# An LSTM over 512 steps in three gate banks instead of two, paired statistics, norms on GpSimd, and a total spread by matmuls

## The chip, the cores and the metric

The kernel runs on one core of one Trainium2 chip. Its time is the device time in microseconds (us) of one execution; less is better. The core's engines are PE (TensorE: matmuls into PSUM, with PEld for loading weights), DVE (VectorE), ACT (ScalarE), POOL (GpSimd) and SP (SyncE, which here issues DMAs). Each engine works through its own queue in order; semaphores tie the queues together.

## The reference, cut to what matters

Two layers are computed on `x` of 32 batches x 512 nodes x 256 features. Everything but the last block (two graph attentions and a state space block) is left as it is by the change. The last block is an LSTM that runs over the 512 nodes, all 32 batches side by side, followed by gated running sums:

```python
def _L1_ffn_ref(x, W_ih, W_hh, b_ih, b_hh, W_lin, b_lin, fw_att, bw_att):   # x is layer-normed
    x_proj = einsum('btd,gd->btg', x, W_ih) + b_ih + b_hh
    def step(carry, xp):
        h, c = carry
        i, f, g, o = split(xp + h @ W_hh.T, 4, axis=-1)
        c = sigmoid(f) * c + sigmoid(i) * tanh(g)
        h = sigmoid(o) * tanh(c)
        return (h, c), h
    lstm_out = scan of step over t
    logits = einsum('bth,lh->btl', lstm_out, W_lin) + b_lin      # two logits
    g = argmax(logits, axis=-1)[..., None]                        # 0 or 1
    w = g * lstm_out
    inc = cumsum(w, axis=1)
    prefix, suffix = inc - w, inc[:, -1:, :] - inc
    return 2.0 * lstm_out + prefix * fw_att + suffix * bw_att
x = x + _L1_ffn_ref(_layernorm(x), ...)
```

`suffix` needs the total over all steps, so a term of every output row is known only when the last step is done.

## The kernel before, in words

Two passes over the batches compute all that comes before the LSTM and leave the result in device memory as `X3` (512 steps x 32 batches x 256). Then `recurrence` runs.

*Layout.* The 256 hidden units are cut into four quarters (`Q` = 4) of 64 (`J`), and a quarter into two halves of 32 (`H`). The 128 partitions hold quarter x batch (4 x 32), so that a gate of one half is 32 columns wide. A step's gates are a PSUM tile pair `pg`: `pg0` has g, f, i of the first half (96 columns), `pg1` has g, f, i of the second half, o of both, and two columns of which the first is the logits' difference (162 columns). `z` is a row of columns of 32: 0 is the state c of the first half, 1 to 3 its gates, 4 the state of the second half, 5 to 7 its gates, 8 and 9 o of both, 10 and 11 tanh(c).

*A step t*, in the order in which the queues of PE, DVE and ACT are written (this part of the kernel is scheduled by hand: program order is queue order on those three engines; SP's and POOL's order is the scheduler's):

- PE: `part(pg, whh, h, ...)` adds h @ W_hh to the gates, for each pair (k, n) of an order, k being the half of h that is the stationary operand and n the gate bank, with one matmul for each of the four quarters. Then `x_part(t + 1, ...)` starts the next step's gates from x. In steps 5, 6, 10 and 11 of a chunk PE also transposes one normed tile of x for the next chunk (`turn`).
- ACT: tanh of `pg0` (L1472), tanh of `pg1` without the logits (L1473), then two tanh(c), one for each half (L1483), a copy of one column (L1485), and, after a transposition, the copy of it out of PSUM (L1356). Sigmoids are made of tanh by scaling the weights by a half.
- DVE: for each half `ab` (L1478) and the new c in `z2` (L1481), then for each half `hh` (L1491) and its 32 x 32 block transposition `h` (L1495), which the next step's matmuls load as weights. Then `g` (L1502, the logit decides whether h counts), one *extra* piece of work, and `pp` (L1508), the running sum.

*Chunks and extras.* 16 steps (`CH`) are a chunk. At its first step the lists of extra work are made; each step takes one entry. Before the change there are 16: four `stats` of the next chunk's x (one tile of 128 rows each: BATCH_NORM_STATS2 and BATCH_NORM_AGGREGATE; the last also gives POOL `rstd_of`, that is `ve` and the power `rs`), two pairs of `norm` (TENSOR_SCALAR on DVE in place, and a POOL memset of the last column), and ten pieces of the former chunk's `results` (128 x 512 adds and products on DVE; the last issues four DMAs on SP that gather the piece into `R`). At a chunk's first step `pp` is also copied (L1510).

*Memory.* `R` (128 partitions x 128 steps x 256) stays in SBUF and collects everything but the total. Its partitions are quarter of the steps x batch.

*The tail.* After the last step `tot` = total x `bw` (128 x 64, quarter x batch on partitions). Sixteen DMAs on three queues lay it out as `tots` (128 x 256, the four quarters of the columns side by side, repeated for the four quarters of the steps). The last chunk's ten result pieces run on DVE, then 17 adds `R` + `tots` in blocks of 2, 6 and 8 steps, each followed by four output DMAs on SP and ACT.

Of the kernel before, what the change touches and what calls it, by code (L numbers as in the profile page):

```python
# [9 lines left out]
F32 = mybir.dt.float32  # L10
# [3 lines left out]
AF = mybir.ActivationFunctionType  # L14
# [5 lines left out]
P = 128  # L20
# [1269 lines left out]
def recurrence(ctx, tc, c, a, X3, wr, out):  # L1290
# [25 lines left out]

    TQ = T // 4
    R = wp.tile([P, TQ, D], F32, name="R")


    NX = CH // 4

    def normalised(t0, out_):


        mv = small.tile([P, NX, 2], F32, tag="mv", name=f"mv{t0}")
        rs = [None]
        xs = []
        for n in range(NX):
            xt = xp_.tile([P, D], F32, tag=f"xt{n}", bufs=1, name=f"xt{t0}_{n}")  # L1330
            nc.sync.dma_start(out=xt, in_=X3[t0 + 4 * n : t0 + 4 * n + 4].rearrange("t b d -> (t b) d"))
            xs.append(xt)

        def stats(n):
            bs = small.tile([P, 6], F32, tag="bs", name=f"bs{t0}_{n}")
            nc.vector.bn_stats(bs, xs[n])
            nc.vector.bn_aggr(mv[:, n, :], bs)  # L1337
            if n == NX - 1:
                rs[0] = rstd_of(nc, small, c, mv[:, :, 1], NX, LN_EPS)

        def norm(n):
            nc.vector.tensor_scalar(
                xs[n], xs[n], mv[:, n, 0:1], rs[0][:, n : n + 1], ALU.subtract, ALU.mult
            )
            nc.gpsimd.memset(xs[n][:, D - 1 :], 1.0)

        def turn(n):
# [10 lines left out]
        return tuple([lambda f=f, n=n: f(n) for n in range(NX)] for f in (stats, norm, turn))  # L1358

    def results(t0, hh, pp):  # L1360

# [56 lines left out]
    def x_part(t, xT):  # L1418

        pg = [psg.tile([P, e - s], F32, tag=f"pg{n}", name=f"pg{n}_{t}") for n, (s, e) in enumerate(PARTS)]  # L1420
        r = (t % G) * GB
        part(pg, wih, [xT[t % CH // G][:, k, r : r + GB] for k in range(DK)], ((0, 0), (1, 0), (0, 1), (1, 1)), True, t == 0)
        return pg

    with tc.manual_schedule(engines={mybir.EngineType.PE, mybir.EngineType.DVE, mybir.EngineType.Activation}):
        nxt = [None] * 2
        stats, norms, turns = normalised(0, nxt)
        for s, e in ((0, nw), (n0, n0 + 2 * J + 1), (nw, n0)):
            nc.sync.dma_start(out=wall[:, s:e], in_=wr[:, s:e])
        for f in stats + norms:  # L1430
            f()
        for f in turns:
            f()()
        extra, turning = [], {}
        pg = x_part(0, nxt)


        z = st.tile([P, 12 * H + 1], F32, tag="z", name="z0")
        for n in range(2):
            nc.vector.memset(z[:, 4 * n * H : (4 * n + 1) * H], 0.0)  # L1440
        pp = ch.tile([P, CH + 1, J], F32, tag="pp", name="pp0")
        nc.vector.memset(pp[:, 0, :], 0.0)
        h = hh = None
        for t in range(T + 1):
            s = t % CH
            last = t == T
            if s == 0 and not last:
                t0 = t
                hh_was, pp_was = hh, pp
                hh = ch.tile([P, CH, J], F32, tag="hh", name=f"hh{t0}")  # L1450
                if t:
                    pp = ch.tile([P, CH + 1, J], F32, tag="pp", name=f"pp{t0}")
                assert not extra and not turning
                xT, nxt = nxt, [None] * 2
                stats, norms, turns = normalised(t0 + CH, nxt) if t0 + CH < T else ([], [], [])
                more = results(t0 - CH, hh_was, pp_was) if t else []
                both = [lambda fs=norms[n : n + 2]: [f() for f in fs] for n in range(0, len(norms), 2)]
                extra = stats + both + more
                turning = {(5, 6, 10, 11)[n]: f for n, f in enumerate(turns)}
            if last:  # L1460

                pg = [None, psg.tile([P, W - 3 * H], F32, tag="pg1", name="pglast")]
                part(pg, whh, h, ((0, 1), (1, 1)), True, True)
            elif t:
                part(pg, whh, h, ((0, 0), (0, 1), (1, 0), (1, 1)), False, True)
            pgs = pg
            if not last:
                if t + 1 < T:
                    pg = x_part(t + 1, xT if t + 1 < t0 + CH else nxt)
                turned = [turning.pop(s)()] if s in turning else []  # L1470

                nc.scalar.activation(z[:, H : 4 * H], pgs[0], AF.Tanh)  # L1472
                nc.scalar.activation(z[:, 5 * H : 10 * H], pgs[1][:, : 5 * H], AF.Tanh)  # L1473
                z2 = st.tile([P, 12 * H + 1], F32, tag="z", name=f"z{t + 1}")
                for n in range(2):
                    c0 = 4 * n * H
                    ab = st.tile([P, 2 * H], F32, tag=f"ab{n}", name=f"ab{n}_{t}")
                    nc.vector.scalar_tensor_tensor(  # L1478
                        ab, z[:, c0 + 2 * H : c0 + 4 * H], 1.0, z[:, c0 : c0 + 2 * H], ALU.add, ALU.mult
                    )  # L1480
                    nc.vector.scalar_tensor_tensor(z2[:, c0 : c0 + H], ab[:, :H], 0.5, ab[:, H:], ALU.mult, ALU.add)  # L1481
                for n in range(2):
                    nc.scalar.activation(z[:, (10 + n) * H : (11 + n) * H], z2[:, 4 * n * H : (4 * n + 1) * H], AF.Tanh, scale=0.5)  # L1483

                nc.scalar.copy(z2[:, 12 * H :], level)  # L1485
                for f in turned:
                    f()
                h = []
                for n in range(2):
                    half = hh[:, s, n * H : (n + 1) * H]  # L1490
                    nc.vector.scalar_tensor_tensor(  # L1491
                        half, z[:, (8 + n) * H : (9 + n) * H], 1.0, z[:, (10 + n) * H : (11 + n) * H], ALU.add, ALU.mult
                    )
                    h.append(st.tile([P, GB], F32, tag=f"h{n}", name=f"h{n}_{t}"))
                    nc.vector.transpose(h[n], half)  # L1495
                z = z2
            if t:

                i = (t - 1) % CH
                p_, h_ = (pp_was, hh_was) if s == 0 and not last else (pp, hh)  # L1500
                g_ = st.tile([P, J], F32, tag="g", name=f"g{t}")
                nc.vector.scalar_tensor_tensor(  # L1502
                    g_, pgs[1][:, 5 * H : 5 * H + 1].to_broadcast([P, J]), level, h_[:, i, :], ALU.is_gt, ALU.mult,
                )
            if extra and not last:
                extra.pop(0)()
            if t:
                nc.vector.tensor_tensor(p_[:, i + 1, :], p_[:, i, :], g_, ALU.add)  # L1508
# [4 lines left out]
        nc.vector.tensor_tensor(tot, pp[:, CH, :], bw, ALU.mult)  # L1513

        tots = wp.tile([P, D], F32, name="tots")
        for n in range(4 * Q):
            tq, q = n // Q, n % Q
            (nc.sync, nc.scalar, nc.gpsimd)[n % 3].dma_start(
                out=tots[tq * GB : (tq + 1) * GB, q * J : (q + 1) * J], in_=tot[q * GB : (q + 1) * GB]
            )  # L1520
        for f in results(T - CH, hh, pp):
            f()
        t0 = 0
        for step in [2, 6] + [8] * (TQ // 8 - 1):
            r = R[:, t0 : t0 + step, :]
            nc.vector.tensor_tensor(r, r, tots.unsqueeze(1).to_broadcast([P, step, D]), ALU.add)  # L1526
            for tq in range(4):
                (nc.sync, nc.scalar)[tq % 2].dma_start(
                    out=out[:, tq * TQ + t0 : tq * TQ + t0 + step, :], in_=r[tq * GB : (tq + 1) * GB]
                )  # L1530
            t0 += step


PERIOD, PIECES = 100234, 49
# [121 lines left out]
```

## Time and profile before

| | |
|---|---|
| median of 3 runs (range) | 3854.9 us (3853.66 to 3856.93) |
| the profiled execution's own time | 3853.91 us |
| its span, first to last instruction | 3852.2 us |
| mean granted PE clock | 0.975 |
| busy in the span: PE, DVE, ACT, POOL | 3417.8, 3256.5, 2403.0, 1510.6 us |
| first activation of the first step (L1472) | 2550.76 us |
| `tot` (L1513), after the last step | 3786.76 us |
| first and last add to `R` (L1526) | 3793.84 to 3829.2 us |

The span is the stretch from the first to the last instruction; the 1.7 us by which the execution is longer lie around it. The recurrence with its tail takes the last third. In it, by windows of the trace (busy us of each engine in a stretch):

| stretch, us | PE | DVE | ACT | POOL | DMA share |
|---|---|---|---|---|---|
| 2900 to 3100 (steady steps) | 171.18 | 187.19 | 98.41 | 9.41 | 0.22 |
| 3787 to 3794 | 0.00 | 6.73 | 0.00 | 2.57 | 0.10 |
| 3794 to 3829 | 0.00 | 35.00 | 0.00 | 0.00 | 0.96 |
| 3829 to 3852.2 | 0.00 | 0.21 | 0.00 | 0.00 | 0.86 |

The groups of the recurrence that the change touches, from the table of costliest groups with shapes kept apart (count, mean of one):

| group | count | mean ns |
|---|---|---|
| L1413 PE matmul, 96 columns, with h | 8128 | 252 |
| L1413 PE matmul, 162 columns, with h | 8128 | 301 |
| L1472 ACT tanh, 128x96 | 508 | 251 |
| L1473 ACT tanh, 128x160 | 509 | 305 |
| L1336 DVE BATCH_NORM_STATS2, 128x256 | 121 | 418 |
| L1337 DVE BATCH_NORM_AGGREGATE | 121 | 182 |
| L1342 DVE TENSOR_SCALAR norm, 128x256 | 124 | 406 |
| L1378 to L1390 DVE result pieces, 128x512 | 320 | 681 |
| L1518 `tots` DMAs | 16 | - |

An fp32 matmul appears as two records in the trace, so a step has 32 matmul records with h and 32 with x. Matmuls that work on different quarters overlap; a "mean of one" is therefore no measure of how often they can follow each other. The timeline of single steps tells that: rows are in order of start, with the length, and in brackets the idle time of that engine before and what released it.

### The profile page before, as it was taken

What the parts mean: (1) busy time and instruction counts of PE and PEld (TensorE: products, weight loads), DVE (VectorE), ACT (ScalarE), POOL (GpSimd) and SP (SyncE); (2) the same over time, 40 slices, a digit from 0 to 9 for tenths busy, and PEclk for the clock granted to TensorE, in tenths of its full rate; (3) what the DMA queues carried; (4) which work ended last, traced back from release to release, by engine and by line L of the source; (5) the groups of instructions that cost most, each with busy time, mean ns of one, the idle gap of its engine ahead of it and who ended that gap; (6) DMA issues with size and microseconds to landing.
All of it is one profiled execution on the core that took longest, in us unless ns stands there. A gap on an engine that the chain in (4) does not pass through costs nothing. (4 is left out here: it accounts for less than half of the span.)

```text
span 3852.2 us, 117182 instructions
## 1 busy us (share of the span) xinstructions
PE 3417.8 (89%) x47370; PEld 2313.5 (60%) x47370; DVE 3256.5 (85%) x10671; ACT 2403.0 (62%) x6434; POOL 1510.6 (39%) x1581
## 2 busy tenths in 40 slices
PE   5999999999999999999999998668888888888882
PEld 3466566556656656655665664446666666666661
DVE  3888888888888888888888886459999999999997
ACT  2777777777777777777777775435454544444441
POOL 3456556555555655655555566710000000000000
PEclk8999999999999999999999998789999999999996
DMA  3322322222223232232223212221222222222226
GB/s 98 89 91 73 101 85 75 94 86 86 83 93 90 72 102 86 72 95 86 86 83 96 87 61 59 82 66 41 44 46 43 46 43 46 43 46 43 46 40 191
DMA packets 271800, 288.76 MB, mean 75 GB/s; under 512 B 151589, under 2 KB 221953, under 8 KB 269073
## 3 DMA queue, kind: packets, MB, share of 16 engines
q1 hardware_dynamic: 265248, 266.96, 25.0%
q10 hardware_dynamic: 3152, 8.76, 0.7%
q8 instruction: 375, 6.14, 0.7%
q0 software_dynamic: 2848, 5.45, 0.5%
q14 instruction: 177, 1.44, 0.1%
HBM read 227.09 MB, written 37.11 MB: 69 GB/s over the span
## 5 line engine op out<-in xcount | busy, mean ns | idle before, releaser
L1413 PE MATMUL pg<-wall,h 128*32 128x96 f32 x16352 | 559.0, 277 | 176.8 <-DVE h L1495 169.4
L1413 PEld LDWEIGHTS pg<-wall,h 128*32 128x32 f32 x16352 | 374.4, 109 | 350.8 <-DVE h L1495 331.9
L1413 PE MATMUL pg<-wall,xTr 128*32 128x96 f32 (+1 forms) x16384 | 549.0, 274 | 0.0
L1413 PEld LDWEIGHTS pg<-wall,xTr 128*32 128x32 f32 x16384 | 447.2, 110 | 5.2 <-issue 0.3
L132 POOL TENSOR_SCALAR ve<-mv 128x4 f32<-128x4 f32 x32 | 6.3, 195 | 1038.5 <-DVE mv L1337 1038.5
L1472 ACT ACTIVATE z<-pg 128x96 f32<-128x96 f32 x512 | 128.7, 251 | 438.9 <-PE pg L1413 438.9
L102 DVE SCALAR_TENSOR_TENSOR w<-rb,colsa,adjT 128x512 f32<-128x512 f32 x512 | 380.4, 778 | 6.0 <-DMA rb<-linea 6.0
L102 DVE SCALAR_TENSOR_TENSOR acc<-px,convw,acc 128x511 f32<-128x511 f32 (+2 forms) x480 | 335.3, 735 | 7.6 <-ACT acc L102 6.4
L1483 ACT ACTIVATE z<-z 128x32 f32<-128x32 f32 x1024 | 234.7, 229 | 168.5 <-DVE z L1481 100.9
L102 ACT ACTIVATE g<-bc,cs 128x128 f32<-128x128 f32 x1024 | 326.0, 399 | 13.1 <-PE py L102 13.1
L102 PE MATMUL px<-mT,win 128*128 128x512 f32 x640 | 307.2, 603 | 0.0
L102 PE MATMUL po<-wc,xh 128*128 128x256 f32 x1024 | 254.3, 392 | 13.5 <-POOL xh L102 8.4
L102 POOL TENSOR_SCALAR ve<-bnmv 128x4 f32<-128x4 f32 x96 | 18.8, 196 | 626.3 <-DVE bnmv L102 607.7
L102 PE MATMUL pav<-w,hb 128*64 128x512 f32 x1024 | 250.1, 608 | 8.0 <-DVE w L102 8.0
L102 PE MATMUL pov<-wb,wv 128*128 128x257 f32 x1024 | 250.5, 392 | 7.0 <-DVE wv L102 5.8
L1495 DVE STREAM_TRANSPOSE h<-hh 128x32 f32<-128x32 f32 x1024 | 216.4, 211 | 34.8
L102 PE MATMUL pz<-mT,win 128*128 128x512 f32 x512 | 245.4, 602 | 0.0
L102 POOL TENSOR_TENSOR rs<-ve,mhalf 128x4 f32<-128x4 f32 (+1 forms) x192 | 237.8, 1239 | 13.3
L1478 DVE SCALAR_TENSOR_TENSOR ab<-z 128x64 f32<-128x64 f32 x1024 | 226.0, 221 | 15.3 <-ACT z L1472 12.0
L102 PEld LDWEIGHTS po<-wc,xh 128*128 128x128 f32 x1024 | 189.5, 193 | 76.6 <-issue 27.0
L1481 DVE SCALAR_TENSOR_TENSOR z<-ab 128x32 f32<-128x32 f32 x1024 | 196.9, 192 | 35.1
L102 POOL TENSOR_SCALAR msk<-adj 128x1024 bf16<-128x1024 int32 x64 | 218.8, 3434 | 13.0 <-DMA adj<-in_adj_dram 7.9
(258 smaller groups left out, 7987.8 us busy)
## 6 DMA issues: line engine op xcount, KB each, us to landing
bc<-line SPq DMA_DIRECT2D x128, 512.0 KB
adj<-in_adj_dram SPq DMA_DIRECT2D x32, 1024.0 KB
rb<-linea SPq DMA_DIRECT2D x64, 512.0 KB
ce<-line SPq DMA_DIRECT2D x64, 384.0 KB
x<-in_x_dram SPq DMA_DIRECT2D x32, 512.0 KB
X<-x SPq DMA_DIRECT2D x32, 512.0 KB
xt<-X SPq DMA_DIRECT2D x128, 128.0 KB
x<-X SPq DMA_DIRECT2D x128, 128.0 KB
```

What stands on the lines that cost most here:

```text
L102: return getattr(getattr(self.nc, engine), op)(*map(real, a), **{n: real(v) for n, v in k.items()})
L132: nc.gpsimd.tensor_scalar(ve, var, scale, eps, ALU.mult, ALU.add)
L1413: nc.tensor.matmul(p[q * GB : (q + 1) * GB, :], lhs[k], w[:, k, q, s:e], start=(start and k == 0), stop=(stop and k == DK - 1),)
L1472: nc.scalar.activation(z[:, H : 4 * H], pgs[0], AF.Tanh)
L1478: nc.vector.scalar_tensor_tensor(ab, z[:, c0 + 2 * H : c0 + 4 * H], 1.0, z[:, c0 : c0 + 2 * H], ALU.add, ALU.mult)
L1481: nc.vector.scalar_tensor_tensor(z2[:, c0 : c0 + H], ab[:, :H], 0.5, ab[:, H:], ALU.mult, ALU.add)
L1483: nc.scalar.activation(z[:, (10 + n) * H : (11 + n) * H], z2[:, 4 * n * H : (4 * n + 1) * H], AF.Tanh, scale=0.5)
L1495: nc.vector.transpose(h[n], half)
```

## The change

Four things are changed in `recurrence`, nothing elsewhere:

- *Three gate banks.* `pg1` is cut into `pg1` (g, f, i of the second half, 96 columns) and `pg2` (o of both and the logits, 66 columns), each a PSUM tile of its own. With h, PE takes both 96-column banks with the first half of h, both with the second, then the narrow bank; with x, bank after bank. ACT has three tanh instead of two.
- *Statistics of two tiles at once.* Two x tiles stand side by side in one buffer, and one BATCH_NORM_STATS2 reads them interleaved (`p k d -> p d k`): its two sets of outputs, for even and odd elements, are then the two tiles' statistics. There is no aggregation; `rstd_of` scales the sum of squares by 1/256. A chunk has two statistics instead of four.
- *Norms on GpSimd.* The same TENSOR_SCALAR as before, issued on POOL instead of DVE. A chunk's extras are thus 2 + 2 + 10 = 14, of which the two pairs of norms put nothing on DVE; the last two steps have no extra, and the results come two steps earlier.
- *The tail.* `sel`, made once at the start by four POOL copies of identity columns, holds for each quarter a 128 x 128 matrix that picks its 32 rows and repeats them four times. Four matmuls of it on `tot` give `tots` in PSUM in place of the sixteen DMAs. The last chunk's result pieces run three at a time after the third and later adds, not ahead of all adds.

```diff
+    sel = wp.tile([P, Q, P], F32, name="sel")
+    for q in range(Q):
+        nc.gpsimd.tensor_copy(
+            sel[:, q, :].rearrange("p (t b) -> p t b", b=GB),
+            c.ident[:, q * GB : (q + 1) * GB].unsqueeze(1).to_broadcast([P, 4, GB]),
+        )
...
         for n in range(NX):
-            xt = xp_.tile([P, D], F32, tag=f"xt{n}", bufs=1, name=f"xt{t0}_{n}")
+            if n % 2 == 0:
+                xt = xp_.tile([P, 2, D], F32, tag=f"xt{n}", bufs=1, name=f"xt{t0}_{n}")
...
-            nc.vector.bn_stats(bs, xs[n])
-            nc.vector.bn_aggr(mv[:, n, :], bs)
-            if n == NX - 1:
-                rs[0] = rstd_of(nc, small, c, mv[:, :, 1], NX, LN_EPS)
+            nc.vector.bn_stats(st_[:, n, :], pairs[n].rearrange("p k d -> p d k"))
+            if n == NX // 2 - 1:
+                rs[0] = rstd_of(nc, small, c, st_.rearrange("p i (k e) -> p (i k) e", k=2)[:, :, 2], NX, LN_EPS, scale=1.0 / D)
...
-            nc.vector.tensor_scalar(
-                xs[n], xs[n], mv[:, n, 0:1], rs[0][:, n : n + 1], ALU.subtract, ALU.mult
+            nc.gpsimd.tensor_scalar(
+                xs[n], xs[n], st_[:, n // 2, 3 * (n % 2) + 1 : 3 * (n % 2) + 2], rs[0][:, n : n + 1], ALU.subtract, ALU.mult
             )
...
-    PARTS = ((0, 3 * H), (3 * H, W))
+    PARTS = ((0, 3 * H), (3 * H, 6 * H), (6 * H, W))
+    ORDER = ((0, 0), (0, 1), (1, 0), (1, 1), (0, 2), (1, 2))
...
-        part(pg, wih, [...], ((0, 0), (1, 0), (0, 1), (1, 1)), True, t == 0)
+        part(pg, wih, [...], ((0, 0), (1, 0), (0, 1), (1, 1), (0, 2), (1, 2)), True, t == 0)
...
-                part(pg, whh, h, ((0, 0), (0, 1), (1, 0), (1, 1)), False, True)
+                part(pg, whh, h, ORDER, False, True)
...
                 nc.scalar.activation(z[:, H : 4 * H], pgs[0], AF.Tanh)
-                nc.scalar.activation(z[:, 5 * H : 10 * H], pgs[1][:, : 5 * H], AF.Tanh)
+                nc.scalar.activation(z[:, 5 * H : 8 * H], pgs[1], AF.Tanh)
+                nc.scalar.activation(z[:, 8 * H : 10 * H], pgs[2][:, : 2 * H], AF.Tanh)
...
-        tots = wp.tile([P, D], F32, name="tots")
-        for n in range(4 * Q):
-            tq, q = n // Q, n % Q
-            (nc.sync, nc.scalar, nc.gpsimd)[n % 3].dma_start(
-                out=tots[tq * GB : (tq + 1) * GB, q * J : (q + 1) * J], in_=tot[q * GB : (q + 1) * GB]
-            )
-        for f in results(T - CH, hh, pp):
-            f()
+        tots = psx.tile([P, DK, P], F32, tag="px", name="tots").rearrange("p k e -> p (k e)")
+        for q in range(Q):
+            nc.tensor.matmul(
+                tots[:, q * J : (q + 1) * J],
+                sel[:, q, :], tot,
+                start=True, stop=True,
+            )
+        rest = results(T - CH, hh, pp)
         t0 = 0
-        for step in [2, 6] + [8] * (TQ // 8 - 1):
+        for n, step in enumerate([2, 6] + [8] * (TQ // 8 - 1)):
             r = R[:, t0 : t0 + step, :]
             nc.vector.tensor_tensor(r, r, tots.unsqueeze(1).to_broadcast([P, step, D]), ALU.add)
...
             t0 += step
+            if n >= 2:
+                for f in rest[:3]:
+                    f()
+                rest = rest[3:]
```

More of the change, by code (lines that the diff above doesn't have):

```diff
@@ L1318, in recurrence @@
     R = wp.tile([P, TQ, D], F32, name="R")
+    sel = wp.tile([P, Q, P], F32, name="sel")
[4 more added lines that the diff above has]
+        )
     NX = CH // 4
     def normalised(t0, out_):
-        mv = small.tile([P, NX, 2], F32, tag="mv", name=f"mv{t0}")
+        st_ = small.tile([P, NX // 2, 6], F32, tag="bs", name=f"bs{t0}")
         rs = [None]
-        xs = []
+        xs, pairs = [], []
         for n in range(NX):
-            xt = xp_.tile([P, D], F32, tag=f"xt{n}", bufs=1, name=f"xt{t0}_{n}")
-            nc.sync.dma_start(out=xt, in_=X3[t0 + 4 * n : t0 + 4 * n + 4].rearrange("t b d -> (t b) d"))
-            xs.append(xt)
-        def stats(n):
-            bs = small.tile([P, 6], F32, tag="bs", name=f"bs{t0}_{n}")
-            nc.vector.bn_stats(bs, xs[n])
-            nc.vector.bn_aggr(mv[:, n, :], bs)
-            if n == NX - 1:
-                rs[0] = rstd_of(nc, small, c, mv[:, :, 1], NX, LN_EPS)
+            if n % 2 == 0:
+                xt = xp_.tile([P, 2, D], F32, tag=f"xt{n}", bufs=1, name=f"xt{t0}_{n}")
+            nc.sync.dma_start(out=xt[:, n % 2, :], in_=X3[t0 + 4 * n : t0 + 4 * n + 4].rearrange("t b d -> (t b) d"))
+            xs.append(xt[:, n % 2, :])
+            if n % 2:
+                pairs.append(xt)
+        def stats(n):
+            nc.vector.bn_stats(st_[:, n, :], pairs[n].rearrange("p k d -> p d k"))
+            if n == NX // 2 - 1:
+                rs[0] = rstd_of(nc, small, c, st_.rearrange("p i (k e) -> p (i k) e", k=2)[:, :, 2], NX, LN_EPS, scale=1.0 / D)
         def norm(n):
-            nc.vector.tensor_scalar(
-                xs[n], xs[n], mv[:, n, 0:1], rs[0][:, n : n + 1], ALU.subtract, ALU.mult
+            nc.gpsimd.tensor_scalar(
+                xs[n], xs[n], st_[:, n // 2, 3 * (n % 2) + 1 : 3 * (n % 2) + 2], rs[0][:, n : n + 1], ALU.subtract, ALU.mult
             )
@@ L1356, in turn @@
             return lambda: nc.scalar.copy(xT, pt)
-        return tuple([lambda f=f, n=n: f(n) for n in range(NX)] for f in (stats, norm, turn))
+        return tuple([lambda f=f, n=n: f(n) for n in range(m)] for f, m in ((stats, NX // 2), (norm, NX), (turn, NX)))
     def results(t0, hh, pp):
@@ L1421, in x_part @@
         r = (t % G) * GB
-        part(pg, wih, [xT[t % CH // G][:, k, r : r + GB] for k in range(DK)], ((0, 0), (1, 0), (0, 1), (1, 1)), True, t == 0)
+        part(pg, wih, [xT[t % CH // G][:, k, r : r + GB] for k in range(DK)], ((0, 0), (1, 0), (0, 1), (1, 1), (0, 2), (1, 2)), True, t == 0)
         return pg
@@ L1460, in recurrence @@
             if last:
-                pg = [None, psg.tile([P, W - 3 * H], F32, tag="pg1", name="pglast")]
-                part(pg, whh, h, ((0, 1), (1, 1)), True, True)
+                pg = [None, None, psg.tile([P, W - 6 * H], F32, tag="pg2", name="pglast")]
+                part(pg, whh, h, ((0, 2), (1, 2)), True, True)
             elif t:
-                part(pg, whh, h, ((0, 0), (0, 1), (1, 0), (1, 1)), False, True)
+                part(pg, whh, h, ORDER, False, True)
             pgs = pg
@@ L1502, in recurrence @@
                 nc.vector.scalar_tensor_tensor(
-                    g_, pgs[1][:, 5 * H : 5 * H + 1].to_broadcast([P, J]), level, h_[:, i, :], ALU.is_gt, ALU.mult,
+                    g_, pgs[2][:, 2 * H : 2 * H + 1].to_broadcast([P, J]), level, h_[:, i, :], ALU.is_gt, ALU.mult,
                 )
@@ L1513, in recurrence @@
         nc.vector.tensor_tensor(tot, pp[:, CH, :], bw, ALU.mult)
-        tots = wp.tile([P, D], F32, name="tots")
-        for n in range(4 * Q):
-            tq, q = n // Q, n % Q
-            (nc.sync, nc.scalar, nc.gpsimd)[n % 3].dma_start(
-                out=tots[tq * GB : (tq + 1) * GB, q * J : (q + 1) * J], in_=tot[q * GB : (q + 1) * GB]
-            )
-        for f in results(T - CH, hh, pp):
-            f()
+        tots = psx.tile([P, DK, P], F32, tag="px", name="tots").rearrange("p k e -> p (k e)")
[4 more added lines that the diff above has]
+                start=True, stop=True,
+            )
+        rest = results(T - CH, hh, pp)
         t0 = 0
-        for step in [2, 6] + [8] * (TQ // 8 - 1):
+        for n, step in enumerate([2, 6] + [8] * (TQ // 8 - 1)):
+            assert not rest or t0 + step <= TQ - CH
             r = R[:, t0 : t0 + step, :]
```

## The prediction

> **What bounds the kernel now.** I read the windows view first: PE, DVE and ACT run in a fixed rhythm from about 2550 us to 3785 us, and after 3787 us only DVE and DMA work. So the change touches 512 steps of one recurrence and a tail. Then the timeline of single steps. A step of the last chunk, which has no extra piece left, DVE, ACT and PE in order of time (start, length, idle before and its releaser):
>
> ```profile
> 3773.78 0.22 DVE L1508 TENSOR_TENSOR pp<-pp,g 128x64 f32<-128x64 f32 x1
> ...
> 3774.15 0.25 ACT L1472 ACTIVATE z<-pg 128x96 f32<-128x96 f32 x1 [0.96 <-PE pg L1413]
> ...
> 3774.43 0.30 ACT L1473 ACTIVATE z<-pg 128x160 f32<-128x160 f32 x1
> 3774.43 0.23 DVE L1478 SCALAR_TENSOR_TENSOR ab<-z 128x64 f32<-128x64 f32 x1 [0.43 <-ACT z L1472]
> ...
> 3774.69 0.19 DVE L1481 SCALAR_TENSOR_TENSOR z<-ab 128x32 f32<-128x32 f32 x1
> ...
> 3774.92 0.59 ACT L1483 ACTIVATE z<-z 128x32 f32<-128x32 f32 x2 [0.19 <-DVE z L1481]
> ...
> 3775.40 0.21 DVE L1495 STREAM_TRANSPOSE h<-hh 128x32 f32<-128x32 f32 x1
> ...
> 3775.67 1.09 PE L1413 MATMUL pg<-wall,h 128*32 128x96 f32 x32 [0.43 <-DVE h L1495]
> ...
> 3776.55 0.25 ACT L1472 ACTIVATE z<-pg 128x96 f32<-128x96 f32 x1 [0.96 <-PE pg L1413]
> ```
>
> This is a loop of dependences, 2.40 us round (3774.15 to 3776.55): 1.52 us from the first activation to PE's first matmul with h, 0.88 us from there to the next activation. DVE waits 0.43 us for ACT, PE 0.43 us for DVE. In every other chunk all 16 steps carry an extra piece (4 statistics, 2 pairs of norms, 10 pieces of results). Such a step is as long, but for another reason:
>
> ```profile
> 3011.87 0.68 DVE L1387 TENSOR_TENSOR m<-pp,wall 128x512 f32<-128x512 f32 x1
> ...
> 3012.47 0.22 DVE L1508 TENSOR_TENSOR pp<-pp,g 128x64 f32<-128x64 f32 x1
> ...
> 3012.64 0.23 DVE L1478 SCALAR_TENSOR_TENSOR ab<-z 128x64 f32<-128x64 f32 x1
> ```
>
> No idle time stands before `ab`: DVE is just free when ACT's result comes (3012.36 + 0.25 + 0.03 = 3012.64). An elementwise DVE instruction lets the next one start some 0.08 us before its end (0.68 long, next after 0.60), so `ab` could have begun at 3012.47 + 0.22 - 0.08 = 3012.61: 0.03 us of slack, no more. First-activation starts give 38.53 us per chunk: 2.40 us for all steps but the first extra of a chunk (2.508, it also copies `pp`) and the fourth (2.42).
>
> The tail:
>
> ```profile
> 3786.76 0.23 DVE L1513 TENSOR_TENSOR tot<-pp,wall 128x64 f32<-128x64 f32 x1
> 3787.02 4.67 SPq L1518 DMA_DIRECT2D tots<-tot  x6
> ...
> 3793.84 35.38 DVE L1526 TENSOR_TENSOR R<-R,tots 128x512 f32<-128x512 f32 x17
> ...
> 3794.55 48.39 ACTq L1528 DMA_DIRECT2D out_dram<-R  x34
> ```
>
> Adds end at 3829.2, the span at 3852.2: from 3794.55 on the output DMA decides (305 GB/s between 3794 and 3829), and for 7 us before it hardly anything is moved.
>
> **Order of the gates on PE.** [...] In the step that starts at 3011.48 the fours start at 3011.48, .58, .66, .80 (first half of h: two of 96 columns, two of 162), then .94, 3012.02, .11, .24 (second half), then x at 3012.38. So a four of 96 costs 0.082 us, one of 162 0.137, and the first after a wait 0.024 more. The second half of h was transposed at 3011.78, and its weights could be loaded from 3011.84, but it queues until .94. The last 96 four starts 3012.02, lasts 0.25, and ACT starts 0.065 later, 3012.36. After the change the first half needs four fours of 96: 3011.48, .58, .665, .747, free at .83; the second half starts at its own readiness, 3011.84, its second four at .944, ACT at .944 + 0.246 + 0.065 = 3012.255. That is **0.10 us earlier**; the loop becomes 2.30 us. The narrow fours (66 columns) would cost 0.055 us by the slope of the other two; nothing in the trace is so narrow, so the upper bound is 0.082 (what 96 cost) and I take 0.055, as streaming explains both rows. The x part gets the same split: 8 x 0.082 + 4 x 0.055 = 0.88, as now.
>
> **A third activation.** f, i, g of the second half come 0.17 us after those of the first, o 0.39 us after (four narrow fours plus two of 96). At L1473 and L1483 in the first step the next ACT instruction started 0.20 us after one of 0.30, so ACT is free by about 0.51; the first tanh(c) needs it at 0.77. Nothing on the path; if the three ran end to end (0.25 + 0.25 + 0.22, and gaps) it would be 0.02 to 0.05 late. I take nothing.
>
> **What a step gains.** Without an extra: 0.10. With one of 0.68 us DVE decides, 2.365 us: 0.035. Statistics of two tiles are one BATCH_NORM_STATS2 of 512 elements; the row of 256 is 0.418, and TENSOR_TENSOR goes from 0.22 (64 elements) to 0.68 (512), 1.03 ns an element, so 0.418 + 0.264 = 0.68, which occupies 0.60 where 0.418 and the 0.182 aggregation occupied 0.55. So the copying step gets 0.05 longer (2.56), the second statistics step is 2.365, two norm steps and two empty ones are 2.30, ten result steps 2.365. Per chunk: +0.05 - 0.035 - 4 x 0.10 - 10 x 0.035 - 0.02 (the old 2.42) = -0.755. Thirty chunks -22.7, the first -1.4 (12 steps without extras), the last -0.95: **-25.0 us**. Lower bound of this gain: the DVE slack is nothing, and 11 x 0.035 x 31 = 12 us are lost of it.
>
> **Norms on GpSimd.** Four TENSOR_SCALAR 128x256 per chunk; POOL rows of the kind are 1.497 (512 wide) and 0.552 (128 wide), so 0.87 between. With `rs` (1.01) and the four memsets (0.17) they start 1.4 us after the second statistics end and finish some 4.2 us later, in step 4; the first transposition is in step 5, so PE's new wait for POOL is met. POOL's queue holds nothing else here. The statistics now wait for two loads at once; SP issues these right behind the transposition that frees the tile (3001.85), five steps or more ahead, and the gather's DMAs go out two steps earlier than before, behind nothing. But they collide with DVE. Of the operations that are to run beside them, this pair shows it:
>
> ```profile
> 221.27 1.51 POOL L102 TENSOR_SCALAR em<-ov 128x512 f32<-128x512 f32 x1
> 221.42 0.49 DVE L102 SCALAR_TENSOR_TENSOR off<-bnmv,rs 128x4 f32<-128x4 f32 x1
> ```
>
> `off` is 0.163 us in the median; here it ends 0.64 after POOL's start, so it could begin 0.48 after it, and `xh`, two inputs in SBUF too, that starts 0.56 after is not late. By the 128-wide case in the trace (freed after 0.18) and this one a 256-wide norm blocks DVE for its first 0.28 us. Placed by the offsets above, the four begin near 1.4, 2.3 (next `ab`), 1.1 (next `hh`) and 2.2 us after an `ab`: the first hits nothing, the others up to 0.28, 0.27, 0.18. Bounds 0 and 4 x 0.28 = 1.1 per chunk; I take 0.4, half of the placed sum and a little: 31 x 0.4 = **+12.4 us** (0 to +34). [...]
>
> **Tail.** Sixteen small DMAs are replaced by four matmuls of `sel` on `tot` (64 columns, some 0.8 us with their wait, from the 0.76 us of `pglast`'s sixteen), so the first add starts at 3787.8 instead of 3793.84, 6.0 earlier. The ten result pieces (6.7 us) come between the adds: at full rate an 8-step block of 1.05 MB leaves in 3.2 to 3.4 us, and three blocks in a row take DVE 2.28 + 2.1 = 4.4, so the DMA starves 1 to 2 us before the gather's own 0.5 MB fills in. SP's gather DMAs stand behind five blocks of outputs and are needed only 20 us later. **-4.5 us** (-3 to -6). POOL builds `sel` (4 copies, 128 wide, under 0.55 each) in the 17.7 us it idled before the first `ve`. The first chunk's norms on POOL (0.87 + 0.1 each) replace 0.35 on DVE, but PE's transpositions there were paced at 1.15 us by ACT's copy: **+0.3** (-0.5 to +1).
>
> **Sum.** -25.0 + 12.4 - 4.5 + 0.3 = -16.8 on the profiled execution's 3853.9 us (span 3852.2 and 1.7 around it): **3837 us**. The median of the runs is 3854.9, 1.0 above; I leave that.
>
> **Rivals.**
> *Norms hold DVE for all their length* (slower). For it: `ce` on POOL, 1.00 us, kept `came` on DVE waiting 0.84. Against: that is a two-input POOL instruction, and the norm's kind let go after a third. If three collisions a chunk cost 2.0 us in all: -25 + 62 - 4.2 = +33, 3887 us. It decides from 0.95 us per chunk ((25 + 4.2) / 31).
> *Narrow fours cost as much as those of 96.* Then PE has 8 x 0.027 = 0.22 us more per step, which matters in the four steps with a transposition. There (h from 2999.47) the transpositions start at 3001.38 and .55; with 0.11 for 128 columns and the 0.09 that passed between x's last columns and the first of them, PE is free for h at 3001.75, 2.28 after the step's start. That becomes 2.50 instead of 2.365, +17 us: 3854 us, no change. Against it: four weight loads are issued in 0.027 us and a first four is delayed by 0.024 only.
> *DVE has no slack in steps with extras*: 12 us of the gain are lost, 3849 us. For it: `ab` starts within 0.03 us of DVE's freedom, and that 0.08 overlap is read off one pair of forms.
>
> **How the numbers follow.** Forecast 0.64, DVE held 0.15, narrow fours 0.08, no slack 0.13. About 0.2% (7.7 us) can be told from no change here. Faster than 3847.2: the forecast but where the collisions reach 0.72 per chunk (0.61) and a part of the last rival (0.05), 0.66; within: narrow fours and the rest, 0.17; slower 0.17. The range takes the bounds of the collisions and of the slack: low -25 - 6 - 0.5 = 3822, less 4 if DVE's overlap is larger; high -25 + 34 - 3 + 1 = 3861. So 3818 to 3860.
>
> **What would show it.** Right: first activations 2.30 us apart in empty steps and 2.36 to 2.37 in result steps, PE's idle time before the second half of h, no `tots` DMAs, `R` adds from some 1 us after `tot`. Wrong: `ab` or `hh` longer than 0.3 us beside a POOL norm in more than three places a chunk; idle time of ACT's first tanh(c) behind the o activation; transposition steps over 2.40; an output DMA that ends no earlier.

## The result, and the profile after

The changed kernel takes 4094.94 us (median of 4 runs, 4093.95 to 4096.23); the kernel before took 3855.77 us beside it. The ratio is 1.062, with a 95% interval of 1.060 to 1.064: 239 us slower, where 18 us faster was forecast.

Read by stages, nearly all of it lies in the 512 steps. From the first activation of the first step to that of the last the changed kernel needs 1474.8 us, the kernel before 1233.0: +241.8. The first of these activations comes 2.8 us later, the stretch from the last one to the end is 2.3 us shorter, and the sum, 242.3, is the difference of the spans (4094.5 and 3852.2). A step lasts 2.886 us in the mean where it lasted 2.413, and the steps differ from each other: the medians of the sixteen places in a chunk lie between 2.52 and 3.22, where they were all 2.40 but for two (2.51 and 2.42).

First the page of the changed kernel: instructions by engine, the queue that brings instructions (packets, MB, share), the chain that ended last, and the two matmul groups of the recurrence (count, busy us, mean ns, idle before and its releaser).

```profile
PE 3501.5 (86%) x63746; PEld 2456.7 (60%) x63746; DVE 3227.4 (79%) x10351; ACT 2423.4 (59%) x6946; POOL 1653.5 (40%) x1708
...
q8 instruction: 503, 8.24, 0.9%
...
PE 21%; issue 8%; DVE 7%; ACT 1%; DMA 0%; POOL 0%; DVEq 0%; SPq 0%; ACTq 0%; POOLq 0%
...
L1421 PE MATMUL pg<-wall,xTr 128*32 128x96 f32 (+1 forms) x24576 | 629.9, 238 | 177.3 <-issue 172.4
L1421 PE MATMUL pg<-wall,h 128*32 128x96 f32 x24528 | 627.0, 240 | 157.7 <-issue 94.9
```

The same of the page of before:

```profile
PE 3417.8 (89%) x47370; PEld 2313.5 (60%) x47370; DVE 3256.5 (85%) x10671; ACT 2403.0 (62%) x6434; POOL 1510.6 (39%) x1581
...
q8 instruction: 375, 6.14, 0.7%
...
DVE 27%; PE 3%; issue 2%; DMA 1%; ACT 1%; SPq 0%; DVEq 0%
...
L1413 PE MATMUL pg<-wall,h 128*32 128x96 f32 x16352 | 559.0, 277 | 176.8 <-DVE h L1495 169.4
L1413 PE MATMUL pg<-wall,xTr 128*32 128x96 f32 (+1 forms) x16384 | 549.0, 274 | 0.0
```

Three things are to be seen. The chain that was DVE's is now PE's. PE's idle time in front of the x matmuls went from none to 177 us, of which 172 are "issue": time in which the engine waited for nothing that the profile shows. And the third bank raised the number of PE instructions: per step 24 matmuls with h and 24 with x in place of 16 and 16, each of them two weight loads and two matmuls in the records, so 192 instructions a step where there were 128. The queue named "instruction" explains the link. Loads and matmuls are 127,492 after and 94,740 before, and the queue brought 503 and 375 packets of 16 KB (8.24 MB in 503): 32,752 instructions more with 128 packets more, 255.9 to a packet. So one packet holds 256 PE instructions of 64 bytes, an estimate from these counts.

The timeline of a step shows where PE stands:

```profile
3103.48 0.52 PE L1421 MATMUL pg<-wall,h 128*32 128x96 f32 x10 [0.28 <-DVE h L1504]
...
3104.83 0.81 PE L1421 MATMUL pg<-wall,h 128*32 128x96 f32 x32 [0.83 <-issue]
...
3105.42 0.25 ACT L1480 ACTIVATE z<-pg 128x96 f32<-128x96 f32 x1 [2.01 <-PE pg L1421]
...
3106.94 1.05 PE L1421 MATMUL pg<-wall,h 128*32 128x96 f32 x41 [0.29 <-DVE h L1504]
...
3107.74 0.25 ACT L1480 ACTIVATE z<-pg 128x96 f32<-128x96 f32 x1 [0.88 <-PE pg L1421]
```

`h` is there at 3103.48 and PE starts; after ten matmuls it stops, and goes on at 3104.83. The second half of `h` was transposed by 3103.79, so no data is late. The activation comes 1.94 us after PE's first matmul with h. One step later nothing interrupts the matmuls, and it comes 0.80 us after: close to what the prediction had (0.88 less 0.10). Between 2650 and 3700 us of the trace PE makes 260 such stops (over 0.3 us without the start of a PE instruction, put down to "issue"; 0.99 us in the mean), and 275 instruction packets start. From one stop to the next it is 255 PE instructions in the median, and a stop ends 2.47 us (median) after the start of a packet.

### The profile page after: what moved, and what is told of

It reads as the page before. It is cut to its first block, busy times and chain, and to the rows that moved or that the text cites. A ratio compares the mean times of both kernels' runs of the same rounds, so it can differ in the third digit from the quotient of the medians.

```text
span 4094.5 us, 150238 instructions
## 1 busy us (share of the span) xinstructions
PE 3501.5 (86%) x63746; PEld 2456.7 (60%) x63746; DVE 3227.4 (79%) x10351; ACT 2423.4 (59%) x6946; POOL 1653.5 (40%) x1708
## 3 DMA queue, kind: packets, MB, share of 16 engines
q8 instruction: 503, 8.24, 0.9%
## 5 line engine op out<-in xcount | busy, mean ns | idle before, releaser
L1421 PE MATMUL pg<-wall,xTr 128*32 128x96 f32 (+1 forms) x24576 | 629.9, 238 | 177.3 <-issue 172.4
L1421 PE MATMUL pg<-wall,h 128*32 128x96 f32 x24528 | 627.0, 240 | 157.7 <-issue 94.9
L1421 PEld LDWEIGHTS pg<-wall,h 128*32 128x32 f32 x24528 | 510.0, 109 | 257.9 <-issue 137.9
L1421 PEld LDWEIGHTS pg<-wall,xTr 128*32 128x32 f32 x24576 | 536.3, 110 | 213.7 <-issue 208.3
```

The lines of the kernel that those rows point to most:

```text
L1421: nc.tensor.matmul(p[q * GB : (q + 1) * GB, :], lhs[k], w[:, k, q, s:e], start=(start and k == 0), stop=(stop and k == DK - 1),)
```

## The experiments

Ten kernels were run in three groups, each beside the kernel before. Theory F: PE's instructions come too late, because a step has 192 of them. Rival N: the norms on GpSimd hold DVE. Rival W: the third bank itself (a third activation, shorter matmuls) makes the steps long.

**Two banks, everything else of the change.** The banks, their order and the activations are those of before; 128 PE instructions a step.

```diff
-    PARTS = ((0, 3 * H), (3 * H, 6 * H), (6 * H, W))
+    PARTS = ((0, 3 * H), (3 * H, W))
```

> The changed kernel with the two gate banks of before (128 PE instructions a step instead of 192); paired statistics, norms on GpSimd and the tail stay. Theory F (PE runs out of instructions: each 256 of them is one 16 KB instruction fetch, and PE stands about 1 us at the end of a block): no PE idle time by issue inside the steps, first activations 2.40 us apart, 3845 to 3865 us. Rival N (norms on GpSimd hold DVE): most of the 240 us loss stays, over 4000 us.

3865.2 us, ratio 1.0034 (1.0025 to 1.0044). The loss of 239 us is gone but for some 12. What is left lies at three places of a chunk: the step that copies `pp` (2.59 us, before 2.51) and the two steps with norms (2.58 and 2.53, before 2.40 and 2.42). All others are 2.40. In these rows of the trace (POOL first, then DVE) a norm holds DVE:

```profile
3026.08 2.46 POOL L1349 TENSOR_SCALAR xt<-xt,bs,rs 128x256 f32<-128x256 f32 x2
...
3028.56 1.22 POOL L1349 TENSOR_SCALAR xt<-xt,bs,rs 128x256 f32<-128x256 f32 x1
...
3029.80 1.28 POOL L1349 TENSOR_SCALAR xt<-xt,bs,rs 128x256 f32<-128x256 f32 x1
```

```profile
3026.24 0.46 DVE L1515 TENSOR_TENSOR pp<-pp,g 128x64 f32<-128x64 f32 x1
3026.90 0.23 DVE L1485 SCALAR_TENSOR_TENSOR ab<-z 128x64 f32<-128x64 f32 x1 [0.20 <-ACT z L1479]
...
3027.57 0.35 DVE L1488 SCALAR_TENSOR_TENSOR z<-ab 128x32 f32<-128x32 f32 x1
...
3028.85 0.34 DVE L1515 TENSOR_TENSOR pp<-pp,g 128x64 f32<-128x64 f32 x1
...
3030.11 0.35 DVE L1488 SCALAR_TENSOR_TENSOR z<-ab 128x32 f32<-128x32 f32 x1
```

`pp` takes 0.46 and 0.34 us instead of 0.22, the new c in `z` twice 0.35 instead of 0.19. The four norms start at 3026.08, 3027.28, 3028.56 and 3029.80, and each makes one DVE instruction 0.12 to 0.24 us longer; these end 0.62 to 0.66 us after their norm's start. So a norm lets DVE go after some 0.4 us (0.64 less the 0.2 that such an instruction takes by itself), long before its end; it is 1.25 us long.

**The three banks alone, on the kernel before.**

```diff
-    PARTS = ((0, 3 * H), (3 * H, W))
+    PARTS = ((0, 3 * H), (3 * H, 6 * H), (6 * H, W))
```

> The kernel before with the three gate banks alone. F: the whole loss comes with them, 4080 to 4110 us, one gap by issue for each 256 PE instructions. N: under 3860 us, since DVE keeps its norms.

4072.41 us, ratio 1.0568 (1.0547 to 1.0589); steps of 2.840 us, and 243 stops of 0.97 us in the mean between 2650 and 3700 us, again 255 PE instructions apart in the median. N falls as the main cause. F and W are both left.

**Sixteen small matmuls more a step, two banks.** They are four columns wide, go into a PSUM tile of their own, and nobody reads it: again 192 PE instructions, but neither a third bank nor a third activation.

```diff
+        for n in range(16):
+            q = n % Q
+            nc.tensor.matmul(spare[q * GB : (q + 1) * GB, 0:4], xT[...][:, 0, r : r + GB], wih[:, 0, q, 0:4], start=True, stop=True)
```

> The kernel before with 16 more matmuls of 4 columns in each step (64 PE instructions, 192 in all), behind the x part, into a PSUM tile that nobody reads; gates, waits and activations as before. F: the count alone costs, over 4000 us. Rival W (it is the third bank: its waits, its narrow matmuls or the third activation): PE has over 0.4 us idle in a step for the added 0.2 us, so 3855 to 3875 us.

4074.74 us, ratio 1.0574 (1.0553 to 1.0595): the same loss as with three banks. W falls: the loss needs no third bank. The table of groups shows the same idle time, in front of matmuls that depend on nothing new:

```profile
L1427 PEld LDWEIGHTS spare<-wall,xTr 128*32 128x32 f32 x16384 | 282.3, 111 | 105.2 <-issue 102.9
L1427 PE MATMUL spare<-wall,xTr 128*32 128x4 f32 x16384 | 274.0, 174 | 92.1 <-issue 91.5
```

**The change with three banks, but 128 PE instructions a step.** What the x part leaves out stands in its expectation.

```diff
-        part(pg, wih, [...], ((0, 0), (1, 0), (0, 1), (1, 1), (0, 2), (1, 2)), True, t == 0)
+        part(pg, wih, [...], ((0, 0), (0, 1)) + (((0, 2),) if t == 0 else ()), True, t == 0)
```

> The changed kernel with the x part thinned to 128 PE instructions a step: x is multiplied with its first 128 features alone and for the two wide banks alone (this part of the computation, the bias with it, is left out). The third bank, the order of the gates and the three activations stay. F: no gaps by issue, first activations 2.30 to 2.37 us apart, 3825 to 3860 us. W: over 4000 us.

3849.46 us, ratio 0.999 (0.998 to 1.0001). Three banks are not slow in themselves: against two banks with the same statistics, norms and tail the span is 15 us shorter (3847.2 and 3862.0), and 12.8 of these lie in the steps (1231.9 us from the first step's first activation to the last step's, where two banks need 1244.8). The x part is also only half as long here; what that alone brings was not tested. A step without extra work in this trace:

```profile
3770.41 0.25 ACT L1480 ACTIVATE z<-pg 128x96 f32<-128x96 f32 x1 [0.88 <-PE pg L1421]
...
3771.93 1.13 PE L1421 MATMUL pg<-wall,h 128*32 128x96 f32 x48 [0.86 <-DVE h L1504]
...
3772.74 0.25 ACT L1480 ACTIVATE z<-pg 128x96 f32<-128x96 f32 x1 [0.89 <-PE pg L1421]
```

From the activation to PE's first matmul it is 1.52 us as before, from there to the next activation 0.81 where it was 0.88. The loop is 2.33 us. In these rows the gain is not that of the shorter x part, as PE waits for `h` in both kernels. And the 48 matmul records with h take 1.13 us where 32 took 1.09: PE is hardly busier for being given more and narrower matmuls.

This kernel has a disturbance of its own. In 16 of the first 31 chunks steps of 2.65 to 3.0 us stand among those with norms and transpositions. The windows (columns as in the tail's windows below: after the five engines the granted PE clock) and the timeline of one of them:

```profile
3019.00:3021.00 2.00, 1.49 (x64) 1.22 (x64) 1.62 (x9) 0.97 (x6) 2.00 (x5) 1.00 0.03 8
3022.00:3023.00 1.00, 1.00 (x32) 1.00 (x28) 1.00 (x4) 0.00 (x0) 0.13 (x2) 0.50 0.00 0
...
3021.77 1.95 PE L1421 MATMUL pg<-wall,h 128*32 128x96 f32 x48 [1.07 <-DVE h L1504]
```

The granted clock is 0.50 instead of 1.00 in sixteen stretches of 3.4 us, one in each of these chunks, and apart from the first chunk's start no other step is longer than its place's median by more than 0.1 us. They cost some 10 us. The before kernel, two banks and the changed kernel have no such stretch in their steps; why the clock falls here was not tested.

**How many instructions a step can hold.** Eight, four and twelve of the small matmuls, to tell a late start of the fetch (F) from a limit of rate (L).

The first edit, against the run with sixteen:

```diff
-        for n in range(16):
+        for n in range(8):
```

> The kernel before with eight small matmuls (4 columns each, into a PSUM tile that nobody reads) behind the x part of every step: 160 PE instructions a step where it had 128. Theory F (the instruction fetch comes too late): a fetch begins some 125 PE instructions before the last one that is there, and new ones can be issued 2.4 to 2.5 us after its start. 125 instructions last 0.78 steps here, 1.88 us, so PE lacks 0.55 us per 256 instructions, 0.35 us per step; of such a lack 0.44 of 0.67 us reached the step with sixteen matmuls, so 0.23 us here: 512 steps give +118 us, 3975 us (3930 to 4030), gaps of about 0.5 us once per 256 instructions. Rival L (a limit of rate alone: 256 instructions per 3.74 us, the pace of the fetches with three banks alone): 256 instructions are 1.6 steps, 3.84 us at the old pace, so no loss, 3855 us (up to 3870). Rival S (the added matmuls' own streaming): half of sixteen's 219 us, 3964 us, without gaps.

> The kernel before with four such small matmuls a step: 144 PE instructions a step. Theory F: 125 instructions last 0.87 steps, 2.08 us, so 0.37 us is lacking per 256 instructions (1.78 steps), 0.21 us a step, of which two thirds reach the step: 0.14 us, +70 us, 3925 us (3885 to 3960), gaps of 0.3 to 0.4 us. Rival L (rate alone): no loss, 3855 us. The curve from 128 over 144, 160 and 192 instructions then tells whether there is a threshold near 128, as F has it (128 instructions in 2.40 us just fit), or one near 160.

> The kernel before with twelve small matmuls a step: 176 PE instructions a step. Rule L, as the runs with 128, 144, 160 and 192 suggest it (a step is as long as its work, 2.40 us, or as the supply of its PE instructions, whichever is longer, and 256 come in 3.75 us at best): 176 x 3.75 / 256 = 2.58 us a step, 512 steps give +92 us, 3946 us; by the pace of the changed kernel, 3.82 us, 2.63 us and 3971 us; so 3940 to 3975. Rival S (a fixed price for each added instruction): between the 20 us of eight and the 219 us of sixteen there is no straight line through the 1.5 us of four, but the half way between them would be 3975 us and no wait for supply in the trace that grows with the count.

Eight cost 19.8 us (3874.66, ratio 1.0051, 1.0034 to 1.0068), four nothing that can be told (3856.37, ratio 1.0004, 0.9993 to 1.0014). So F's reckoning from a fixed lead of 125 instructions (+118 and +70) falls. Twelve cost 135 us (3990.05, ratio 1.0351, 1.0332 to 1.0369), above the 85 to 120 expected. A limit of rate comes nearer: it had four right, but no loss for eight (up to 3870) and at most 3975 us for twelve, and missed both. All of them in one table, between 2650 and 3700 us of the trace. The interval is the mean from one instruction packet's start to the next, the next column what it would have been with steps as long as before (interval x 2.413 / step), and the last the stops of PE, as counted above, and their sum:

| kernel | PE instructions a step | step, us | interval of packets, us | at a step of 2.413, us | stops, their sum in us |
|---|---|---|---|---|---|
| before | 128 | 2.413 | 4.75 | 4.75 | 0 |
| four small matmuls | 144 | 2.416 | 4.23 | 4.22 | 1, 0.8 |
| eight | 160 | 2.454 | 3.88 | 3.82 | 31, 18 |
| twelve | 176 | 2.674 | 3.86 | 3.48 | 171, 119 |
| sixteen | 192 | 2.843 | 3.75 | 3.18 | 216, 177 |
| three banks alone | 192 | 2.840 | 3.74 | 3.18 | 243, 236 |
| the change | 192 | 2.886 | 3.82 | 3.19 | 260, 257 |

Interval and step are one measurement seen twice, since a packet is 256 instructions: 192 x 3.82 / 256 gives back the 2.86 us of the change and proves nothing. What tells is that the interval follows the falling column only down to about 3.9 us and then stays between 3.74 and 3.88, and that the stops begin there and grow with the count. From there on the steps follow the packets. This is a mean: single intervals go down to 3.24 to 3.31 us in all seven kernels. The price is not per instruction added: 144 costs nothing that can be told, 160 half a per cent, from there on the step grows by some 0.2 us for sixteen instructions.

**Norms back on DVE**, with two banks, paired statistics and the new tail.

```diff
-            nc.gpsimd.tensor_scalar(
+            nc.vector.tensor_scalar(
```

> The change with the two gate banks of before and with the norms on DVE again; statistics of two tiles at once and the new tail stay. If the norms on GpSimd made the loss that was left with two banks (collisions with DVE), the steps with norms are 2.40 us again, the copying step stays near 2.56 to 2.59 (its statistics are longer), so 38.6 us per chunk where two banks with GpSimd norms had 38.94: 3853 us (3850 to 3856), 12 us under that. Rival: the paired statistics cost it (loads for two tiles at once, later rs): 3860 us or more.

3855.44 us, ratio 1.0003 (0.9994 to 1.0013): 38.62 us per chunk for 38.94. The norms on GpSimd cost 0.32 us a chunk, 9.9 us in 31. The paired statistics cost nothing but in the copying step (2.59 us), and bring next to nothing either (the fourth step is 2.40 us where it was 2.42): steps with and without extra work are 2.40 us long, so the work they save was not on the path.

**The new tail alone, with one result piece behind each add** instead of three, on the kernel before.

```diff
-                for f in rest[:3]:
-                    f()
-                rest = rest[3:]
+                for f in rest[:1]:
+                    f()
+                rest = rest[1:]
```

> The kernel before with the new tail alone, but one result piece behind each add from the third on, not three. My prediction gave the tail -4.5 us (-3 to -6); with two banks it brought only 1.9 from tot to the end (63.5 us for 65.4), where three pieces in a row let the output DMA run dry. If that is the reason, one piece at a time gives the 4 to 5 us: 3850 us (3848 to 3852). Rival: the gather on SP that holds back the outputs behind it is the reason: 1 to 2.5 us, 3852 to 3854 us.

3849.08 us, ratio 0.9987 (0.9978 to 0.9997). From `tot` to the end it takes 61.0 us in the trace, where it was 65.4 before and 63.5 with three pieces at a time. The windows (stretch, length, busy PE, PEld, DVE, ACT, POOL, clock, DMA share, GB/s), first of two banks with the tail as changed, whose `tot` is at 3798.54:

```profile
3806.00:3812.00 6.00, 0.00 (x0) 0.00 (x0) 5.97 (x6) 0.00 (x0) 0.00 (x0) 0.50 0.97 286
3812.00:3818.00 6.00, 0.00 (x0) 0.00 (x0) 5.93 (x7) 0.00 (x0) 0.00 (x0) 0.50 0.94 253
3818.00:3824.00 6.00, 0.00 (x0) 0.00 (x0) 6.00 (x3) 0.00 (x0) 0.00 (x0) 0.50 0.95 255
```

and of one piece behind each add, with `tot` at 3785.27:

```profile
3794.00:3800.00 6.00, 0.00 (x0) 0.00 (x0) 6.00 (x6) 0.00 (x0) 0.00 (x0) 0.50 0.98 307
3800.00:3806.00 6.00, 0.00 (x0) 0.00 (x0) 6.00 (x6) 0.00 (x0) 0.00 (x0) 0.50 1.01 351
3806.00:3812.00 6.00, 0.00 (x0) 0.00 (x0) 6.00 (x5) 0.00 (x0) 0.00 (x0) 0.50 1.00 347
```

With three pieces the output runs at 286 and 253 GB/s, with one at 307 to 351. The third window is not the pieces': from 3818.22 on SP issues the gather, whose packets are small (256 bytes in the traces of before and after), and the rate falls with one piece too (254 GB/s between 3824 and 3830). The missing rate of the second alone is worth some 1.7 us (an estimate: 6 us x 98 / 351), the two kernels differ by 2.5. But the output did not run dry, as the expectation had it: the DMA engines were busy for 0.94 of that window, and a packet, about 5.5 KB in the mean, took 0.33 us in it where it took 0.25 with one piece. Why it takes longer stays open, and since the gather now also stands behind 24 outputs instead of 12, the rival's part was not separated. The last two adds, into the blocks that the gather fills, wait 8.25 us, which the profile puts down to an output DMA; so the next run also moves the gather.

**What paid, together.** Two banks, paired statistics, norms on DVE, no extra in the copying step, the tail of the last run, and the last gather on POOL's queue. The two edits that are new:

```diff
-                extra = stats + both + more
+                extra = [lambda: None] + stats + both + more
...
-                nc.sync.dma_start(
+                (nc.gpsimd if t0 == T - CH else nc.sync).dma_start(
                     out=R[tq * GB : (tq + 1) * GB, ...], in_=x3[q * GB : (q + 1) * GB]
```

> What paid, together: the two gate banks of before, statistics of two tiles at once, norms on DVE, the lists of extra work begun at the second step of a chunk (so that the step that copies pp has no other extra), the new tail with one result piece behind each add and the last gather's DMAs on POOL's queue, where no output stands before them. Expected: 38.45 us per chunk where it was 38.53 before and 38.62 with the statistics in the copying step (31 x 0.08 = 2.5 us), and from tot to the end 57 to 61 us where it was 65.4 and, with the gather behind the outputs, 61.0 (the adds waited 8.25 us there for it): 3846 us (3842 to 3850). Rival: the copying step stays at 2.50 without an extra, as the copy itself makes it long, and the gather on POOL is no earlier: 3850 us or more.

3845.56 us, ratio 0.9976 (0.9965 to 0.9986): 9 us under the kernel before, and 249 under the changed one. All steps are 2.40 us, 38.45 per chunk, and from `tot` to the end it takes 60.3 us. The gather's part is small: it is issued at 3817.46, 3.8 us earlier than in the run before, and the last adds still wait for it,

```profile
3830.45 4.49 DVE L1534 TENSOR_TENSOR R<-R,tots 128x2048 f32<-128x2048 f32 x2 [6.69 <-DMA R<-x]
```

which takes from 3817.46 to 3830.45 to come. That the output DMAs slow it is likely (the DMA share is 0.99 to 1.00 in that time), but not shown.

## Why the prediction was wrong, point by point

**Order of the gates on PE.** This is the step that failed. It priced PE by how long its matmuls stream ("8 x 0.082 + 4 x 0.055 = 0.88, as now") and held "four weight loads are issued in 0.027 us" against a price on each four. Within a burst that is right: 48 records with h took 1.13 us where 32 took 1.09. But the sum had no term for the number of PE instructions, which grows from 128 to 192 a step, and so none for their supply. With the 3.75 us per packet of the sixteen unread matmuls, a kernel without the third bank, that term is 192 x 3.75 / 256 = 2.81 us a step against the 2.30 forecast; measured are 2.886, and the difference of +241.8 us in the steps is nearly all of the loss. Sixteen unread matmuls on the kernel before show it without a third bank; three banks at 128 instructions show the reverse. The page of before would have told what to ask: 47370 loads and as many matmuls, 375 packets, and steps that use up a packet in 4.75 us. What it could not tell is where the limit lies, because nothing in it ran into one.

Its gain itself was there, but smaller: at 128 instructions the empty steps are 2.325 us, not 2.30, as PE's part of the loop shrinks by 0.07 (0.81 for 0.88 us) and not by 0.10.

**A third activation: nothing.** Right: in the thinned kernel tanh of o starts at 3770.80 and ends at 3771.02, and tanh(c) at 3771.18 starts when DVE's c is there.

**What a step gains, -25.0 us.** Never seen in the changed kernel as a whole. At 128 instructions it was -12.8 in the steps against two banks, and some -20 by the medians of a chunk's places (38.31 for 38.94, times 31), which leave out the stretches at half clock: result steps 2.357 (forecast 2.365), the copying step 2.59 (2.56), empty steps 2.325. How much of it the halved x part brings is open.

**Norms on GpSimd, +12.4 us.** Right in size: 9.9 by the chunks, 12 by the two ratios (1.0034 and 1.0003). A norm is 1.25 us long, not 0.87, and holds DVE for some 0.4 us from its start, not 0.28; but a DVE instruction is made only 0.12 to 0.24 us longer by it, as the prediction's placing had it (0 to 0.28). All four norms hit something, 0.68 us in the rows above, where the placing had three hits and 0.73, and 0.32 us of it reaches a chunk. That about half would, was taken without a reason, so the agreement is partly luck. The rival that DVE is held for a norm's whole length fell: DVE instructions end 0.62 to 0.66 us after the start of a norm that is 1.25 us long.

**Tail, -4.5 us.** From `tot` to the end -2.0 with two banks, -2.1 in the changed kernel. `tots` and the first add were early as said (the first add 1.4 us after `tot`, forecast 1.0), but the prediction let the DMA starve for "1 to 2 us" and then run at full rate. The engines did not starve (DMA share 0.97 and 0.94); the rate was 286 and 253 GB/s for the 12 us of the pieces. With one piece behind each add it was -4.4.

**Start, +0.3 us.** +2.8 in the changed kernel, 0.0 with two banks. Neither can be told from chance: in the single traces of the twelve kernels the first activation comes between 2547.80 and 2557.43 us, and the latest is the kernel before with nothing but sixteen small matmuls added.

**The rivals** named three engines and waits, and none of them a resource that has no row among the engines. "Narrow fours cost as much as those of 96" was nearest the place, but it put the price on each four; the price is on the sum of all PE instructions, and only above some 144 to 160 of them in a step of 2.4 us (2.416 us with 144, 2.454 with 160, 2.674 with 176).

## What to carry to other kernels

Splitting a matmul in two doubled its weight loads and matmuls here (one of two banks was split, and 128 PE instructions a step became 192); before doing it in a loop, count the PE instructions per turn and compare with the turn's length. Here 256 of them never came in less than 3.74 us in the mean: a turn of 2.40 us held 144 without loss (ratio 1.0004) and 160 with little (1.0051). The sign was a gap "issue" on PE that came back every 255 instructions in the median, while the mean interval of the instruction queue's packets no longer shrank as instructions were added (3.88 us with 160, 3.74 to 3.82 with 192). Where a split pays by its order, as here (0.81 us for 0.88 from PE's first matmul to the activation), it has to be bought with instructions saved elsewhere in the turn; a full x part with fewer PE instructions was not tried.

## What the runs showed of the hardware

The mean interval of the packets that bring PE's instructions does not fall below 3.74 to 3.88 us in the five kernels with 160 to 192 instructions a step, while a packet itself takes only 1.0 to 1.1 us in the trace. So the packet's transfer alone does not fill the interval. Where PE stops, it goes on some 2.5 us after a packet's start (medians and means from 2.43 to 2.56), and the next packet starts 1.2 us (median) to 1.3 us (mean) after that, when PE has started about half of the new 256 instructions (medians of 113 to 131 in the four kernels with 176 and more). Together these two make up the 3.7 to 3.9 us. What fills the first, what starts the next packet, and why the mean differs by up to 4% from kernel to kernel, stays open. An even limit per instruction is not the explanation: after the stop that ends at 3104.83 in the changed kernel 124 PE instructions (60 matmuls, 64 weight loads) start within 1.1 us, and the idle time before them comes in one piece, 1.04 us of PEld and 0.83 us of PE.
